# One level of Strassen for the linear layer and for the product of the squares, with the sums spread over GpSimd and ScalarE

## The chip, the cores and the metric

The kernel runs on one core of one Trainium2 chip. The metric is device time in microseconds, the median of several executions; beside it one execution was taken with the hardware profiler, and all durations below are from that one. The engines are TensorE (PE in the profile, its weight loads are PEld), VectorE (DVE), ScalarE (ACT), GpSimd (POOL) and SyncE (SP, which here only starts transfers).

## The reference, cut to what matters

x is 1024 x 512, `weight` is 64 x 512 x 512 (e, f, m), `lin_w` is 512 x 512, all float32.

```python
out_lin = x @ lin_w.T + lin_b
xv = einsum('bf,efm->bem', x, weight)
zp = einsum('bf,efm->bem', square(x), square(weight))
return out_lin + 0.5 * sum(square(xv) - zp, axis=1)      # over e
```

The sum of zp over e is the one product square(x) @ (sum over e of square(weight)), 1024 x 512 by 512 x 512, as large as the linear layer. The product xv is 64 times as large, and its squares have to be formed before the sum over e.

## The kernel before, in words

**The large product.** The 512 outputs are taken in 16 groups of 32; with 64 values of e a group is a product of x (1024 x 512) with a 512 x 2048 matrix. Each group is done by two levels of Strassen in Winograd's form: seven outer products (`tree`, once for each of 1, 6, 2, 7, 5, 4, 3 in `ORDER`), each again by seven inner products (`product`, L488 to L495), each of which is two matmuls of a 128 x 128 stationary block with a 128 x 512 moving block. In all that is 16 x 7 x 7 x 2 = 1568 matmuls; the profile counts every float32 matmul as two instructions, so 3136.

**The sums around it.** The sums of x's blocks are made once, at the start, by VectorE (`x_sum`, tile `x_all` with seven slots X1 to X7). The sums of the weights' blocks are made in part by transfers that add (`load_more`, issued from GpSimd), in part by GpSimd (`t` tiles, L472 to L479). Results leave PSUM through ScalarE copies and VectorE additions; GpSimd makes additions between two SBUF tiles (`whole`, L288). The finished block of xv is squared on ScalarE and summed over e on VectorE (`finish`), into a tile `acc` of 32 columns for each group, which is stored to a scratch tensor in DRAM (`acc_dram`). The weights are squared on ScalarE and summed over e on VectorE (`w_squares`) into the tile `w2_sum` (512 x 512).

**The two small products.** At the start the linear layer is done while x's sums are still being made: L338 to L360, 4 contraction blocks x 8 row tiles = 32 matmuls of 128 x 512, contraction block by contraction block as x and `lin_w` arrive, in four PSUM tiles (b1, b3 and the two of the ring b2, each of two banks). The four are copied out by ScalarE and stored to a second scratch tensor, `lin_dram`. At the end the product of the squares is done in the same shape: L631 to L642, eight row tiles of four matmuls. Before it x is loaded again into the weight tiles w11 and w12 and turned into -0.5 times its square by four VectorE instructions (L604 to L611); the linear layer's result is added by GpSimd-issued adding transfers onto tiles filled with the bias (L603); `acc` of the 15 stored groups comes back by plain transfers (L599) and is added by VectorE (L613 to L622), that of the last group straight from SBUF (L623 to L626). VectorE then adds PSUM to that (L647) and SP stores each of the eight row tiles (L651).

**The order.** The instructions of every engine are emitted in the order that a planner finds (`Plan.order`): each operation has a cost for each engine, its tiles as dependencies, and PE's order is fixed by keys (`key=`). For the other engines it picks by latest allowed time. Every engine runs its own list strictly in order, waiting on semaphores where it depends on another; DMAs are issued in the same way in SP's list (plain ones) and in POOL's list (adding ones).

Of the kernel before, what the change touches and what calls it, by code (L numbers as in the profile page):

```python
# [12 lines left out]
AF = mybir.ActivationFunctionType  # L13
# [3 lines left out]
P = 128  # L17
G = 2
ORDER = (1, 6, 2, 7, 5, 4, 3)

# [160 lines left out]
def kernel(  # L181
# [138 lines left out]
    for k in range(NK):  # L320
        q, r = divmod(k, KH)
        x0, x1, l = f"oa{q}", f"oa{2 + q}", f"ob{q}"
        nc.sync.dma_start(buf[x0][:, r, :], x_src[:, k, ts(0, H)])
        nc.scalar.dma_start(buf[l][:, r, :], lw_src[:, k, :])
        nc.sync.dma_start(buf[x1][:, r, :], x_src[:, k, ts(1, H)])
        for name in (x0, l, x1):
            landing((name, r), 4.3 + 2.6 * k)


    zero = buf["t1_0"]  # L330
    nc.vector.memset(zero, 0.0)  # L331
    for j in range(2):
        nc.tensor.matmul(  # L333
            buf["b1"][:, j, :], zero[:, 0:P], zero, start=True, stop=True
        )
    plan.add({PE: 4.0}, None, (), ("b1",), key=-2000)

    lin_banks = ["b3", "b1", "b2_0", "b2_1"]  # L338
    for k in range(NK):
        q, r = divmod(k, KH)  # L340
        for g, bank in enumerate(lin_banks):
            h = g // 2
            late = k == NK - 1 and g == 3

            def emit(_, k=k, q=q, r=r, g=g, h=h, bank=bank):
                for j in range(G):
                    nc.tensor.matmul(  # L347
                        buf[bank][:, j, :],
                        buf[f"oa{2 * h + q}"][:, r, ts((g * G + j) % (NB // 2), P)],
                        buf[f"ob{q}"][:, r, :],  # L350
                        start=(k == 0),
                        stop=(k == NK - 1),
                    )

            plan.add({PE: PAIR}, emit, ((f"oa{2 * h + q}", r), (f"ob{q}", r)),
                     (bank,), key=PLACE[5] + 0.5 if late else -1000 + 4 * k + g)
    for g, bank in enumerate(lin_banks):
        o = ("ob2", "ob3", "c_0", "c_1")[g]
        act(buf[o], buf[bank], None, (bank,), (o,))
        dma(lin_dram[:, ts(g, G), :], buf[o], (o,), (("lind", g),))  # L360

    def block4(i):
        return buf[f"X{i}"][:, 0:4, :].rearrange("p (k q) b -> p k (q b)", k=2)

# [10 lines left out]
    for i, n in ((1, "A11"), (2, "A12"), (4, "A22")):  # L375
        act(block4(i), a_ap(n), None, a_parts(n), (f"X{i}",))

    def x_sum(writes, o, a, b, kind, reads, size):

        if kind != "-a - b":  # L380
            costs, emit = two_input(DVE, o, a, b, kind == "a - b", size)
        else:
            costs = two_input(DVE, o, a, b, True, size)[0]

            def emit(_):
                nc.vector.scalar_tensor_tensor(o, a, -1.0, b, ALU.mult, ALU.subtract)

        plan.add(costs, emit, reads, writes, both=True)

    for i, a, b, kind in (  # L390
        (5, "A22", "A21", "a - b"),
        (6, "X5", "A11", "-a - b"),
        (7, "A11", "A21", "a - b"),
        (3, "X6", "A12", "-a - b"),
    ):
        x_sum((f"X{i}",), block4(i), a_ap(a), a_ap(b), kind, a_parts(a, b), 1024)
    for lo, hi in ((0, 1), (1, 7)):
        a11, a21, a12, a22, s1, s2, s4 = (x_all[:, lo:hi, s, :] for s in range(7))
        names = tuple(f"X{i + 1}" for i in range(lo, hi))
        for o, a, b, kind in (  # L400
            (s1, a21, a22, "a + b"),
            (s2, s1, a11, "a - b"),
            (s4, a12, s2, "a - b"),
            (a21, a11, a21, "a - b"),
        ):
            x_sum(names, o, a, b, kind, names, Q * (hi - lo))
    for n in a_buf.values():
        plan.add({SP: 0.0}, None, (), (n,) + tuple((n, r) for r in range(KH)))
    for n in ("ob0", "ob1"):
        plan.add({SP: 0.0}, None, (), (n, (n, 0), (n, 1)))  # L410
# [11 lines left out]
    def load_more(n, src, reads=()):  # L422

        plan.add(
            {POOL: 0.9},
            lambda _: nc.gpsimd.dma_start(buf[n], src, accum_op=ALU.add),
            (n,) + reads, (n,), land=2.5, move=5.5,
        )
# [39 lines left out]
    def tree(s, g, i):  # L468
# [16 lines left out]
        def product(p, b, first):  # L485
            op, name = rhs[p]

            def emit(_):  # L488
                for j in range(G):
                    nc.tensor.matmul(  # L490
                        buf[b][:, j, :], buf[f"X{i}"][:, SLOT[p], ts(j, P)], op,
                        start=first, stop=True, skip_group_check=True,
                    )

            plan.add({PE: PAIR}, emit, (name, f"X{i}", b), (b,), key=7 * s + PLACE[p])  # L495
# [4 lines left out]
        def target(pos):  # L500
            return f"{TARGET[i]}{pos}"

        def early(pos):

            return pos == 3 and i in (2, 7, 4, 3)
# [56 lines left out]
    for g in range(NG):  # L562
# [6 lines left out]
        for idx, i in enumerate(ORDER):  # L569
# [10 lines left out]
            tree(7 * g + idx, g, i)  # L580
        if g + 1 < NG:
            names = tuple((acc_name[g], *k) for k in acc_parts)
            dma(acc_dram[:, :, ts(g, MG)], buf[acc_name[g]], names, names + (("accd", g),))


    for n in ("w11", "w12", "w21", "T1", "T2", w(NG, "w22")):
        for c in range(2):
            buf[n, c] = buf[n][:, c]
        plan.add({SP: 0.0}, None, (), (n, (n, 0), (n, 1)))
    xe = {(h, q): (("w11", "w12")[h], q) for h in range(2) for q in range(2)}  # L590
    last = acc_name[NG - 1]
    edge = M - MG
    acc_all = tuple((n, c) for n in ("T2", w(NG, "w22")) for c in range(2))
    lin_all = tuple((n, c) for n in ("w21", "T1") for c in range(2))
    for (h, q), n in xe.items():
        dma(buf[n], x_src[:, ts(q, KH), ts(h, H)], (), (n,))
    for g in range(NB // G):
        n, a = lin_all[g], acc_all[g]
        dma(buf[a][:, :, 0:edge], acc_dram[:, ts(g, G), 0:edge],  # L599
            tuple(("accd", x) for x in range(NG - 1)), (a,))  # L600
        for j in range(G):
            dma(buf[n][:, j, :], lin_b.partition_broadcast(P), (), (n,), 1.0)
        load_more(n, lin_dram[:, ts(g, G), :], (("lind", g),))  # L603
    for n in xe.values():  # L604
        plan.add(
            {DVE: 1.24},
            lambda _, x=buf[n]: nc.vector.scalar_tensor_tensor(  # L607
                x, x, -0.5, x, ALU.mult, ALU.mult
            ),
            (n,), (n,),  # L610
        )  # L611

    def add_acc(g, lo, hi, a, reads):  # L613
        l = buf[lin_all[g]][:, :, lo:hi]
        plan.add(
            {DVE: 0.15 + 1.09 * (hi - lo) / N},
            lambda _: nc.vector.scalar_tensor_tensor(l, a, 0.5, l, ALU.mult, ALU.add),
            reads + (lin_all[g],), (lin_all[g],),
        )

    for g in range(NB // G):
        add_acc(g, 0, edge, buf[acc_all[g]][:, :, 0:edge], (acc_all[g],))  # L622
    for g in range(NB // G):  # L623
        rows = {0: (2, 3), 1: (4, 5)}[g // 2]
        reads = tuple((last, i, 2 * (g % 2) + c) for i in rows for c in range(2))
        add_acc(g, edge, M, buf[last][:, ts(g, G), :], reads)  # L626
# [3 lines left out]
    w2_parts = tuple(("w2", row, m * MI) for row in range(2) for m in range(M // MI))  # L630
    for g, bank in enumerate(("b3", "b1", "b2_0", "b2_1")):  # L631
        o = acc_all[g]
        h = g // 2
        for j in range(G):
            def emit(_, bank=bank, g=g, h=h, j=j):
                for k in range(NK):
                    nc.tensor.matmul(  # L637
                        buf[bank][:, j, :],
                        buf[xe[h, k // KH]][:, k % KH, ts((g * G + j) % (NB // 2), P)],
                        w2_sum[:, k, :],  # L640
                        start=(k == 0), stop=(k == NK - 1),
                    )  # L642

            plan.add({PE: 2 * PAIR}, emit, (xe[h, 0], xe[h, 1]) + w2_parts,
                     ((bank, j),) + ((bank,) if j == 0 else ()), 
                     key=last_key - 0.5 if (g, j) == (0, 0) else last_key + 1 + 2 * g + j)
            costs, emit = two_input(  # L647
                DVE, buf[o][:, j, :], buf[bank][:, j, :], buf[lin_all[g]][:, j, :], False, 512
            )
            plan.add(costs, emit, ((bank, j), lin_all[g], o), ((o, "out", j),))  # L650
            dma(out_dst[:, g * G + j, :], buf[o][:, j, :], ((o, "out", j),), ())  # L651
# [35 lines left out]
```

## Time and profile before

| | |
|---|---|
| median of 3 runs | 1414.77 us (1414.66 to 1415.5) |
| the profiled execution | 1415.29 us, of which its span from first to last instruction is 1413.5 us |
| PE busy | 1405.5 us, 3268 instructions |
| VectorE, GpSimd, ScalarE busy | 1079.4, 1012.5, 680.6 us |
| linear layer (L347) | 64 instructions, 28.5 us busy, from 5.04 to 35.1 us |
| product of the squares (L637) | 64 instructions, 27.8 us busy, from 1379.3 to 1408.7 us |
| an addition of 128 x 1024 | VectorE 1.22 us, GpSimd 2.36 us at the least |
| an addition of 128 x 512 | GpSimd 1.27 us |
| starting an adding transfer of 1 MB | 0.87 us of GpSimd at the least |

In a line of groups or of the timeline the columns are: (start and) duration in us, engine, line of the code, operation, tile written <- tiles read, shapes, how many (x), and in square brackets how long the engine was idle before and what released it. Where several instructions follow one another they are merged into one line with their count.

### The profile page before, as it was taken

To read this page: it belongs to the slowest core of one execution; us is meant where nothing else is said; L and a number is where in the kernel's file an instruction comes from. 1 tells how busy PE (TensorE), PEld (TensorE's weight loads), DVE (VectorE), ACT (ScalarE), POOL (GpSimd) and SP (SyncE) were. 2 spreads that over 40 slices of the span, in tenths; PEclk is the share of its full clock that TensorE was granted. 3 is DMA by queue.
4 is the path that set the end of the run, shared out by engine and by line. 5 is a ranking of instruction groups with operands and counts; after the bars stand their busy time and mean duration, and the time that the engine had idled before them with its cause. 6 is when DMAs were issued, how large, how long until landed. Compare 5 with 4: busy or idle time off the path is not lost.

```text
span 1413.5 us, 10316 instructions
## 1 busy us (share of the span) xinstructions
PE 1405.5 (99%) x3268; PEld 621.4 (44%) x3268; DVE 1079.4 (76%) x933; ACT 680.6 (48%) x696; POOL 1012.5 (72%) x693
## 2 busy tenths in 40 slices
PE   9999999999999999999999999999999999999998
PEld 4444444444444444444444444444444444444443
DVE  6588695877959687696867869687795968769785
ACT  2446364544636355463544636454463644536331
POOL 3686786968678686777958678686877868678660
PEclk9999999999999999999999999999999999999999
DMA  7184472917538183572908447292663818357263
GB/s 267 60 205 122 119 182 67 241 53 175 156 95 206 48 221 91 140 184 79 230 30 195 136 116 185 59 246 56 166 165 90 212 41 213 107 126 181 54 178 90
DMA packets 47638, 197.55 MB, mean 140 GB/s; under 512 B 19040, under 2 KB 20064, under 8 KB 25696
## 3 DMA queue, kind: packets, MB, share of 16 engines
q0 software_dynamic: 11664, 82.84, 30.4%
q1 hardware_dynamic: 35344, 112.99, 22.7%
q10 hardware_dynamic: 576, 1.05, 0.2%
q8 instruction: 27, 0.44, 0.1%
q14 instruction: 27, 0.22, 0.1%
HBM read 173.93 MB, written 6.16 MB: 127 GB/s over the span
## 4 chain that ended last, share of the span: by engine, by line
PE 99%; DVE 1%; issue 0%; DVEq 0%
PE b L490 95%; PE b L347 2%; PE b L637 2%; DVE w L607 0%; PE b L333 0%; DVE oa L284 0%; DVE acc L305 0%; DVE w22a L284 0%; DVEq L683 0%; DVE t L331 0%
## 5 line engine op out<-in xcount | busy, mean ns | idle before, releaser
L490 PE MATMUL b<-t,x_all 128*128 128x512 f32 x1792 | 806.1, 592 | 1.7 <-DVE oa L284 1.7
L490 PEld LDWEIGHTS b<-t,x_all 128*128 128x128 f32 x1792 | 340.3, 190 | 430.7 <-issue 423.6
L490 PE MATMUL b<-w,x_all 128*128 128x512 f32 x768 | 358.1, 592 | 0.0
L284 POOL TENSOR_TENSOR t<-w 128x512 f32<-128x512 f32 x128 | 172.3, 1346 | 163.0 <-PE b L490 93.4
L296 ACT COPY p<-b 128x1024 f32<-128x1024 f32 x160 | 160.9, 1006 | 151.2 <-PE b L490 151.2
L490 PEld LDWEIGHTS b<-w,x_all 128*128 128x128 f32 x768 | 145.9, 190 | 183.7 <-issue 172.7
L284 POOL TENSOR_TENSOR t<-w,t 128x512 f32<-128x512 f32 x128 | 174.1, 1360 | 66.7 <-PE b L490 66.5
L298 ACT ACTIVATE oa<-oa 128x1024 f32<-128x1024 f32 x128 | 133.7, 1057 | 152.7 <-DVE oa L284 152.0
L305 DVE TENSOR_REDUCE acc<-oa 128x16 f32<-128x1024 f32 x128 | 153.8, 1212 | 36.8 <-ACT oa L298 36.8
L490 PE MATMUL b<-T,x_all 128*128 128x512 f32 x384 | 180.4, 592 | 0.0
L305 DVE TENSOR_REDUCE w_sum<-wsq 128x16 f32<-128x1024 f32 x128 | 154.8, 1211 | 25.3 <-ACT wsq L298 25.3
L296 ACT COPY b<-b 128x1024 f32<-128x1024 f32 x112 | 111.9, 999 | 124.7 <-PE b L490 124.7
L284 DVE TENSOR_TENSOR oa<-b,p 128x1024 f32<-128x1024 f32 x96 | 117.1, 1220 | 37.7 <-PE b L490 37.7
L298 ACT ACTIVATE wsq<-w 128x1024 f32<-128x1024 f32 x96 | 98.0, 1056 | 74.3 <-DVE w_sum L305 70.0
L284 POOL TENSOR_TENSOR t<-T 128x512 f32<-128x512 f32 x64 | 91.7, 1433 | 58.1 <-issue 33.1
L284 DVE TENSOR_TENSOR ob<-b,p 128x1024 f32<-128x1024 f32 x48 | 58.6, 1221 | 71.8 <-PE b L490 71.8
L490 PEld LDWEIGHTS b<-T,x_all 128*128 128x128 f32 x384 | 73.0, 190 | 91.8 <-issue 91.8
L298 ACT ACTIVATE c<-c 128x1024 f32<-128x1024 f32 x64 | 66.0, 1056 | 95.4 <-POOL c L284 67.5
L284 DVE TENSOR_TENSOR p<-b,p 128x1024 f32<-128x1024 f32 x80 | 97.6, 1220 | 18.0 <-PE b L490 18.0
L284 POOL TENSOR_TENSOR t<-T,t 128x512 f32<-128x512 f32 x64 | 81.3, 1271 | 20.2 <-PE b L490 20.2
L284 POOL TENSOR_TENSOR c<-oa,p 128x1024 f32<-128x1024 f32 x32 | 89.3, 2791 | 0.1
L284 POOL TENSOR_TENSOR ob<-ob,p 128x1024 f32<-128x1024 f32 x32 | 89.3, 2789 | 0.0
(58 smaller groups left out, 1320.6 us busy)
## 6 DMA issues: line engine op xcount, KB each, us to landing
w<-weight SPq DMA_DIRECT2D x48, 1024.0 KB, 4.9
T<-weight POOLq DMA_DIRECT2D x45, 1024.0 KB, 8.6
T<-weight SPq DMA_DIRECT2D x30, 1024.0 KB, 7.1
w<-weight POOLq DMA_DIRECT2D x16, 1024.0 KB, 11.1
w<-T POOLq DMA_DIRECT2D x16, 1024.0 KB, 6.9
w22a<-weight SPq DMA_DIRECT2D x8, 1024.0 KB, 8.1
w22b<-weight SPq DMA_DIRECT2D x8, 1024.0 KB, 8.1
oa<-xT SPq DMA_DIRECT2D x8, 256.0 KB, 5.4
```

Of the source, the lines that this page charges most:

```text
L284: f(o, a, b)
L296: nc.scalar.copy(o, i)
L298: nc.scalar.activation(o, i, func)
L305: lambda _: nc.vector.tensor_reduce(o, i.rearrange("p a (m e) -> p a m e", e=E), axis=AX.X, op=ALU.add),
L347: nc.tensor.matmul(buf[bank][:, j, :], buf[f"oa{2 * h + q}"][:, r, ts((g * G + j) % (NB // 2), P)], buf[f"ob{q}"][:, r, :], start=(k == 0) ...
L490: nc.tensor.matmul(buf[b][:, j, :], buf[f"X{i}"][:, SLOT[p], ts(j, P)], op, start=first, stop=True, skip_group_check=True,)
L637: nc.tensor.matmul(buf[bank][:, j, :], buf[xe[h, k // KH]][:, k % KH, ts((g * G + j) % (NB // 2), P)], w2_sum[:, k, :], start=(k == 0), st ...
```

## The change

Both small products are done by one level of the same seven-product scheme: x in blocks of 512 x 256, the right-hand matrix in blocks of 256 x 256. A block product (`big_product`) is 8 matmuls of a 128 x 128 stationary block with a moving block of 256 columns, so 56 matmuls of 256 columns stand in place of 32 of 512.

- Linear layer: the left-hand blocks and their sums are those which the large product needs anyway; x and `lin_w` are loaded in another order (first the upper half of x, all four contraction blocks; the lower half after it). The sums of `lin_w`'s blocks (`column_sums`) are four VectorE additions. Two ScalarE copies carry product 1 from PSUM to PSUM, five more bring products out, and three VectorE additions (`lin_last`) complete the results. The last half of product 7 comes after the first inner product of the first tree, as a part of the linear layer did before.
- The first group takes its trees in the order 1, 2, 6, 7, 5, 4, 3.
- Product of the squares: x is squared by ScalarE. Its four block sums (128 x 1024) and the four sums of `w2_sum`'s blocks (128 x 512) are made by GpSimd, into slots of `x_all` that are no longer used. The factor -0.5 moves to the additions at the end.
- Each stored `acc` is halved in place by ScalarE (128 x 256, once for each of the 15 groups), and added to the output tile by four adding transfers from `acc_dram`, where plain transfers and VectorE additions stood. The linear layer's result is added by four such transfers as before. These eight move blocks of four rows of 256 columns per partition, 1 KB at a piece, where the four before moved two rows of 512 columns, 4 KB in one piece.
- VectorE: seven additions from PSUM of 128 x 1024, the last in two halves. The output is stored in five transfers.

```diff
 ORDER = (1, 6, 2, 7, 5, 4, 3)
+ORDER_0 = (1, 2, 6, 7, 5, 4, 3)
...
+    for h, order in enumerate(((0, 1, 2, 3), (2, 3, 0, 1))):
+        for at, k in enumerate(order):
+            q, r = divmod(k, KH)
+            n, l = f"oa{2 * h + q}", f"ob{q}"
+            nc.sync.dma_start(buf[n][:, r, :], x_src[:, k, ts(h, H)])
...
+            if h == 0:
+                nc.scalar.dma_start(buf[l][:, r, :], lw_src[:, k, :])
...
+    def column_sums(engine, b, t, reads, names):
+
+        for k, x, y, r in (
+            (1, b[1], b[0], (0, 1)),
+            (2, b[3], t[1], (3, "t1")),
+            (3, b[3], b[1], (3, 1)),
+            (4, b[2], t[2], (2, "t2")),
+        ):
+            costs, emit = two_input(engine, t[k], x, y, engine == POOL, 512)
...
+    def big_product(bank, lhs, rhs, first, keys, by_k=False):
+
+        (a, a_names), (b, b_names) = lhs, rhs
+        steps = [(u, [k]) for k in range(KH) for u in range(G)]
+        for (u, ks), key in zip(steps if by_k else [(u, range(KH)) for u in range(G)], keys):
+            def emit(_, u=u, ks=ks):
+                for j in range(2):
+                    for k in ks:
+                        nc.tensor.matmul(
+                            buf[bank][:, u, ts(j, HM)],
+                            a[:, k, ts(2 * u + j, P)],
+                            b[:, k, :],
+                            start=first and j == 0 and k == 0,
+                            stop=k == KH - 1,
+                            skip_group_check=True,
+                        )
...
+    lin_product(1, "b2_0", True, -1000, by_k=True)
+    for u in range(G):
+        act(buf["b2_1"][:, u, :], buf["b2_0"][:, u, :], None, (("b2_0", u),), (("b2_1", u),), 0.56)
+    lin_product(2, "b2_0", False, -999, by_k=True)
+    act(buf["ob2"], buf["b2_0"], None, both_halves("b2_0"), ("ob2",))
+    lin_store("ob2", 0, 0)
+    lin_product(4, "b1", True, -998)
+    act(buf["c_0"], buf["b1"], None, both_halves("b1"), ("c_0",))
+    lin_product(5, "b3", True, -997)
+    act(buf["c_1"], buf["b3"], None, both_halves("b3"), ("c_1",))
+    lin_product(6, "b2_1", False, -996)
+    act(buf["ob3"], buf["b2_1"], None, both_halves("b2_1"), ("ob3",))
+    lin_product(3, "b3", False, -995)
+    act(buf["c_2"], buf["b3"], None, both_halves("b3"), ("c_2",))
+    lin_last("ob3", "c_2", -1)
+    lin_store("ob3", 0, 1)
+    lin_product(7, "b2_1", False, -994, last=PLACE[5] + 0.5)
+    lin_last("c_1", "b2_1", -1)
...
-            dma(acc_dram[:, :, ts(g, MG)], buf[acc_name[g]], names, names + (("accd", g),))
+            a = buf[acc_name[g]]
+            plan.add({ACT: 0.4}, lambda _, a=a: nc.scalar.mul(a, a, 0.5), names, names)
+            dma(acc_dram[:, :, ts(g, MG)], buf[acc_name[g]], names, names + (("accd", g),), 0.9)
...
+    for h, c in blocks:
+        n, rows = lin_all[h, c], ts(h, NB // 2)
+        for j in range(NB // 2):
+            dma(quarter(buf[n])[:, j, :], lin_b[ts(c, HM)].partition_broadcast(P), (), (n,), 0.5)
+        load_more(n, lin_dram[:, rows, ts(c, HM)], (("lind", h, c),), 2.7, quarter)
+        load_more(n, acc_dram[:, rows, c * HM:c * HM + edge[c]],
+                  tuple(("accd", x) for x in range(NG - 1)), 2.7,
+                  lambda ap, w=edge[c]: quarter(ap)[:, :, 0:w])
     for n in xe.values():
-        plan.add(
-            {DVE: 1.24},
-            lambda _, x=buf[n]: nc.vector.scalar_tensor_tensor(
-                x, x, -0.5, x, ALU.mult, ALU.mult
-            ),
-            (n,), (n,),
-        )
+        act(buf[n], buf[n], AF.Square, (n,), (n,), 1.07)
...
+    for p, a, b, kind in (
+        (5, a21, lhs[4], "a + b"),
+        (6, 5, lhs[1], "a - b"),
+        (7, lhs[1], a21, "a - b"),
+        (3, lhs[2], 6, "a - b"),
+    ):
...
+        x_sum((f"R{i}", f"X{i}", f"Y{i}"), block4(i), a[0], b[0], kind, a[1] + b[1], 1024, POOL)
...
+    column_sums(POOL, w2_quad, zt, w2_names, zt_names)
...
+    zp_product(1, bank_a, True, -0.9)
+    for u in range(G):
+        act(buf[bank_2][:, u, :], buf[bank_a][:, u, :], None, ((bank_a, u),), ((bank_2, u),), 0.56)
+    zp_product(5, bank_3, True, 1)
+    add_part(1, 1, bank_3, False)
+    zp_product(6, bank_2, False, 2)
+    add_part(0, 1, bank_2, False)
+    zp_product(2, bank_a, False, 3)
+    add_part(0, 0, bank_a, True)
+    zp_product(7, bank_2, False, 4)
+    add_edge(1)
+    add_part(1, 1, bank_2, True)
+    add_part(1, 0, bank_2, False)
+    zp_product(3, bank_3, False, 5)
+    add_edge(0)
+    add_part(0, 1, bank_3, True)
+    zp_product(4, bank_b, True, 6)
+    add_part(1, 0, bank_b, True, True)
```

Here `lin_product` and `zp_product` call `big_product` with the named product's two operands, `lin_store` stores a block to `lin_dram`, `add_part` adds -0.5 times a PSUM tile to the output tile and stores it where told, and `add_edge` adds half of the last group's `acc`. `b1`, `b3`, `b2_0` and `b2_1` (`bank_a`, `bank_3`, `bank_2`, `bank_b`) are the four PSUM tiles.

## The prediction

> **What bounds the kernel now.** I read the page's busy times first, then the chain that ended last, then who waited for whom, then the timeline at both ends. The page and the chain:
>
> ```profile
> PE 1405.5 (99%) x3268; PEld 621.4 (44%) x3268; DVE 1079.4 (76%) x933; ACT 680.6 (48%) x696; POOL 1012.5 (72%) x693
> ...
> PE 99%; DVE 1%; issue 0%; DVEq 0%
> ```
>
> ```profile
> 5.24 26.44 PE b L347 x60
> 31.68 1.72 PE b L490 x4
> 33.40 1.72 PE b L347 x4
> 35.11 1294.38 PE b L490 x3016
> ...
> 1330.66 4.99 DVE w L607
> ...
> 1338.05 41.44 PE b L490 x96
> 1379.49 3.43 PE b L637 x8
> 1382.92 1.72 PE b L490 x4
> 1384.64 24.05 PE b L637 x56
> ```
>
> PE is the bound from end to end, at a granted clock of 1.00: 3016 instructions in 1294.38 us are 429.2 ns each, and nothing else fits between them. So a matmul removed from PE's list is worth its full 0.86 us, as long as PE is then not kept waiting. The only wait of PE behind its first instruction is one of 1.7 us in the waits:
>
> ```profile
> PE b L490 <- DVE oa L284: 1.7, 1, 1.7
> ```
>
> It stands at 1338.05. VectorE was late because one of its four squarings (L607) took 4.99 us instead of 1.2 to 1.3, beside GpSimd additions.
>
> **Matmuls: the gain.** Each small product goes from 64 instructions of 512 columns to 56 matmuls = 112 instructions of 256 columns. The trace has none of 256. From below the price is half of 429.2 = 214.6 ns. From above it is set by the weight loads, which double in number:
>
> ```profile
> 1338.02 0.30 PEld L490 LDWEIGHTS b<-t,x_all 128*128 128x128 f32 x2 [2.51 <-POOL t L284]
> 1338.56 0.19 PEld L490 LDWEIGHTS b<-t,x_all 128*128 128x128 f32 x1 [0.24 <-issue]
> ```
>
> A load takes 0.19 us, and two together cover 0.30, so the second starts 0.11 behind the first; in steady work a load starts with the matmul ahead of it and has 0.24 us to spare. With 256 columns it would still have 0.215 - 0.19 = 0.025. The Trainium skill speaks against this (TensorE: Matmul & The Clock Gate): its "Back-to-back issue gap" says that in a stream of loads and matmuls the spacing is set by both (81 ns where the isolated gap is 56, for 128 columns), and its "The mechanism" that a load overlaps a matmul only in another row group. The second would put 0.11 us on each of 2 x 112 instructions, 24 us, and the change would lose; but then 429.2 ns could not hold here either, since two passes of 512 at 2.4 GHz already fill 426.7. The first would put some 25 ns on each, 5.6 us in all. The page's isolated form, N/2.4 + 2.5, fits 429.2, so for two passes of 256 I take 215.8 ns: 112 x 0.2158 = 24.17 us a product.
>
> - Linear layer before: 26.44 + 1.72 = 28.16, of which 28.16 - 64 x 0.4292 = 0.69 belongs to the first instructions at a slow clock (their loads take 0.34 instead of 0.19 until 6.6 us). After: 24.17 + 0.69 = 24.86. Gain 3.30.
> - Squares before: 3.43 + 24.05 = 27.48. After 24.17. Gain 3.31.
> - The 1.71 us wait: the squarings leave VectorE for ScalarE (4 x 1.06; it is idle for 26.8 of the 46.6 us from 1338.05 to 1384.64). Gain 1.71.
>
> Together 8.32 us.
>
> **The start: can PE be fed?** Before, no matmul but the first waited for data; now PE goes through the upper half of x and all of `lin_w` in 7 us.
>
> ```profile
> 7.71 1.28 ACT L296 ACT_TABLE_LOAD   x1 [7.71 <-DMA oa<-xT]
> 9.09 1.23 DVE L284 TENSOR_TENSOR x_all<-oa,oa 128x1024 f32<-128x1024 f32 x1 [7.68 <-DMA oa<-xT]
> ```
>
> These two waits end when 768 KB and 1024 KB have come on SP's queue, with as much on ACT's beside it; the moved bytes by microsecond (27, 215, 303, 393, 332, 330, 404 KB from 1 us on) put both 0.9 us behind the data. By this rule the contraction blocks land at 4.8, 6.2, 7.7 and 9.0 us. PE needs them at 5.2, 7.6, 9.4 and 11.1: no wait. Product 2 must wait for ScalarE to carry product 1 away: x's first block lands at 6.2, table load 1.28, copy 1.05, free at 8.5; PE's first half is done at 8.5, the copy (0.56) ends near 9.2, PE wants it at 9.4; the second half 0.15 us ahead likewise. Product 4 (12.8) waits for the fourth sum of `lin_w`: VectorE makes three 0.42 us sums behind ScalarE's copy and three of 0.69, 8.5 + 1.3 + 2.1 = 11.9. Product 5 needs a sum of x at 13.5 (PE 16.3), 6 and 3 theirs at 16.0 and 17.2 (PE 19.7, 23.2). Later VectorE stands at the addition behind product 7 until 31.9 with half of T2's sum queued behind it; T2's sum then ends near 34.3, GpSimd's first difference from it near 35.6, and PE takes that at 45.5. The new tree order asks for w21 second, which lands before T2 is summed. I put 0.2 us down (0 to 1.5), for the margins of 0.15.
>
> The 15 halvings of `acc` (about 0.4 us each, by ScalarE's 1.0 us for 1024) lie in ScalarE's idle half; the stored results and bias loads in DMA time before 1360. If a halving came ahead of a PSUM copy that PE waits for, it would cost 0.4 once.
>
> **The end: GpSimd.** Here lies the risk. Its list before:
>
> ```profile
> 1365.71 1.30 POOL L284 TENSOR_TENSOR t<-w22b,t 128x512 f32<-128x512 f32 x1
> 1366.93 1.74 POOL L426 DMA_DIRECT2D T<-lind  x2
> 1368.07 3.00 POOL L284 TENSOR_TENSOR oa<-p,oa 128x1024 f32<-128x1024 f32 x1
> 1377.53 2.37 POOL L284 TENSOR_TENSOR ob<-p,ob 128x1024 f32<-128x1024 f32 x1 [6.47 <-DVE p L284]
> 1379.84 1.77 POOL L426 DMA_DIRECT2D w<-lind  x2
> ```
>
> It is done at 1381.6 with gaps. I walked the new list against PE's (in the old times, where PE's last stretch begins at 1384.64). From 1345.4, when the sum of w21's columns can start (PE takes it at 1348.6; its adding transfer is started near 1333.4 and needs at most 11.3 us as before), GpSimd has no gap: 10 additions of 512 at a pitch of 1.24, 10 of 1024 at 2.32 (1355.22, 1357.54, 1359.86 in the timeline), 7 transfer starts at 0.87. That is 12.4 + 23.2 + 6.1 = 41.7, so the last addition of the last tree ends at 1387.1 instead of 1379.9. Behind it hang ScalarE's square (1.06), VectorE's reduction (1.21), `add_edge` (0.3) and the addition that empties b2_0 (1.22); block product 7 writes b2_0 at 1384.64 + 3 x 3.45 = 1395.0. So GpSimd may be done as late as 1391.0: 3.9 us to spare. All operands that PE takes from it before (sums of x and of `w2_sum`) end by 1381, ahead of their products.
>
> Unknown is what starting a transfer in 1 KB pieces costs. The near rows: 0.87 us for 1 MB in 8 KB pieces and 0.84 for 512 KB in 4 KB pieces, both 128 pieces; now there are 512. From below 0.87; from above, all of it per piece, 3.5. The Trainium skill points both ways: DMA: Bandwidth & Descriptors ("Anatomy of one DMA — SWDGE (gpsimd) path") says that many descriptors go out before more of them cost time, but Perfetto Trace Analysis ("DMA Instruction — SWDGE (GPSIMD)") says that the row ends when the last one is written, so the row is just this work. With 0.87 GpSimd ends at 1387.1, with 3.5 at 1387.1 + 7 x 2.63 = 1405.5, and PE waits 14.5 us. The row has no trend with bytes, so I stay near it: 1.3, that is +3.0. Also the adding transfer of `acc` must wait on the queue until that of the linear layer into the same tile has landed (6.5 to 10.0 us from its start before; in the walked list the second's turn comes 7.7 us behind the first's start): +1, between 0 and 2.3. GpSimd then ends at 1391.1, at the limit. I put 0.4 us down.
>
> The tail behind the last matmul keeps its two VectorE halves (1.29 us) and the last 256 KB store, now in 1 KB instead of 2 KB pieces: 0.2 (0 to 0.5).
>
> **Sum.** 8.32 - 0.2 - 0.4 - 0.2 = 7.5 us. The span 1413.5 becomes 1406.0, the profiled execution 1415.29 becomes 1407.8. It stood 0.52 above the median, so the median 1414.77 becomes 1407.3; I say 1407.2.
>
> **Rivals.**
> 1. GpSimd is late by some us (starts of 1.5 to 2.5 us, or waits on landings): everything beyond 3.9 us of lateness is PE's wait. At 2.0 a start: 7.9 + 1 - 3.9 = 5.0 us in place of the 0.4, so 1411.8; in all 1408.5 to 1414. For it: the list without gaps. Against: the 3.9.
> 2. The weight loads show: 5.6 us by the 25 ns above, 1412.8, or a part of it. For it: only 0.025 us to spare. Against: a load needs the array for 0.11.
> 3. No gain at all but a loss: the same GpSimd starts at 2.8 us or more. The 7.9 us that are left of the gain are used up at 2.4 us (7 x 1.54 + 1 - 3.9), and from 2.8 it is slower by over 0.2%; at 3.5, 18.4 + 1 - 3.9 = 15.5 us and 1422. For it: four times as many pieces. Against: two sizes with the same row.
> 4. The start stalls 1 to 3 us (table load, copies, landings): 1408 to 1410.
> 5. All margins hold and the stores cost nothing: 8.3 us, 1406.5, or a little lower.
>
> **How the numbers follow.** Forecast with case 5: 0.58, within 1405.7 to 1408.4. Rival 1: 0.22; rival 2: 0.08; rival 3: 0.05; rival 4: 0.07. What this kernel's measurement can tell from no change is about 0.2%, 2.8 us. Range 1405.4 to 1411.5: above it lie rival 3, most of 2 and the end of 1, 0.14 in all. Faster 0.90, same 0.05, slower 0.05.
>
> **What would show it.** In the changed profile: the block products' matmuls (`big_product`) at 0.216 us each (the chain's pieces of the two products 24 to 25 us); no wait of PE on VectorE near 1336; the first tree reached 3.3 us earlier; GpSimd's starts of `lind` and `accd` transfers with their own duration; a wait of PE, if any, in the last 25 us on VectorE or GpSimd. Starts above 2.0 us, or 256-column instructions above 0.24 us, would make the prediction wrong.

## The result, and the profile after

The changed kernel takes 1408.97 us (median of 6 runs, 1408.17 to 1409.48), the kernel before beside it 1414.97 us (6 runs, 1414.66 to 1415.86). The ratio is 0.9956 with a 95% interval of 0.9943 to 0.9969: 6.0 us faster where 7.5 were forecast. The number lies in the range (1405.4 to 1411.5), but 1.8 us above the point, and above the 1405.7 to 1408.4 that the forecast's own case was given. So at least one term of the sum was wrong.

The profiled execution is the fastest of the six: 1408.17 us, span 1406.4. That matters below, because it flatters the start of the program. The page's busy times first, then the chain that ended last (start, duration, what):

```profile
PE 1398.7 (99%) x3364; PEld 639.1 (45%) x3364; DVE 1079.7 (77%) x929; ACT 693.4 (49%) x721; POOL 1039.1 (74%) x706
```

```profile
5.05 3.65 PE b L405 x16
...
8.72 0.58 ACT b L299
...
9.35 1.14 PE b L405 x4
...
10.57 0.58 ACT b L299
...
11.19 18.40 PE b L405 x84
29.59 1.72 PE b L580 x4
31.31 1.73 PE b L405 x8
33.03 1342.43 PE b L580 x3128
1375.47 3.45 PE b L405 x16
1378.92 1.72 PE b L580 x4
1380.64 20.93 PE b L405 x96
```

PE is still the bound. The trees (L580) now run from 33.03 to 1375.47 in one piece: the 1.7 us of VectorE in the middle of the old chain is gone. The 256-column instructions (L405) in an unbroken stretch cost 3.45 / 16 = 0.2156 us and 1.73 / 8 = 0.216 us. New on the chain are two ScalarE copies inside the linear layer. The waits say the same (engine and line that waited, for whom, us in total, times, longest):

```profile
PE b L405 <- ACT b L299: 1.4, 2, 0.7
```

These are the two copies of product 1 from PSUM to PSUM that the forecast had ending 0.15 us ahead of PE. The copies' own lines are in the second block; in the first, PE's:

```profile
9.35 1.13 PE L405 MATMUL b<-ob,oa 128*128 128x256 f32 x4 [0.66 <-ACT b L299]
11.19 2.86 PE L405 MATMUL b<-ob,oa 128*128 128x256 f32 x12 [0.71 <-ACT b L299]
```

```profile
8.72 0.57 ACT L299 COPY b<-b 128x512 f32<-128x512 f32 x1 [0.25 <-PE b L405]
10.57 0.57 ACT L299 COPY b<-b 128x512 f32<-128x512 f32 x1 [1.28 <-PE b L405]
```

The first half of product 1 is complete about 0.86 us before the second. Yet the copy of that first half starts at 8.72, behind the last matmul of the whole product (5.05 + 3.65 = 8.70). The copy of the second half, whose data are just as ready at 8.70, starts at 10.57, behind PE's next four instructions (9.35 + 1.14 = 10.49), which only write the other half. ScalarE was not what held it, since its first copy had ended at 9.30. So both copies wait for whatever PE wrote last into the two-bank tile, not for their own half. The semaphore counts in the built program say so too: the first copy waits for all eight matmuls of product 1, the second also for the two that follow.

At the other end, GpSimd's list had been the risk. Its timeline, with the duration that each record shows:

```profile
1342.56 1.29 POOL L516 DMA_DIRECT2D w22a<-lind  x1
1343.39 1.76 POOL L287 TENSOR_TENSOR t<-w,t 128x512 f32<-128x512 f32 x1
...
1376.20 3.85 POOL L516 DMA_DIRECT2D w22a<-accd  x1
1377.00 4.37 POOL L516 DMA_DIRECT2D T<-accd  x1
1377.77 5.97 POOL L287 TENSOR_TENSOR oa<-p,oa 128x1024 f32<-128x1024 f32 x1
1380.09 5.97 POOL L287 TENSOR_TENSOR ob<-p,ob 128x1024 f32<-128x1024 f32 x1
```

The records overlap: the next one begins about 0.8 us behind a transfer start, but from then on every record is longer. An addition of 128 x 1024 shows 2.36 us before the first start, and 5.97 us behind seven of them, 3.65 us more than the 2.32 us pitch. So a start costs 0.8 us of the list's pitch and 0.5 us (3.65 / 7) of a lag that piles up, 1.3 us together. That the lag is real is seen in those who wait: ScalarE's square of the last result but one starts at 1383.78, with the end of that addition's record (1377.77 + 5.97 = 1383.74), and its square of the last one at 1386.10 (1380.09 + 5.97 = 1386.06). What hangs on them is VectorE's work ahead of block product 7. It waits for the first of the two squares, and from there on it has no gap, so the last addition but one sets the time and the last one has about 1 us to spare:

```profile
1384.87 1.22 DVE L308 TENSOR_REDUCE acc<-oa 128x16 f32<-128x1024 f32 x1 [1.99 <-ACT oa L301]
...
1389.59 1.22 DVE L757 SCALAR_TENSOR_TENSOR T<-b,T 128x1024 f32<-128x1024 f32 x1
```

The second line is the addition that empties the PSUM tile for product 7; it ends at 1390.81. PE's timeline of block products 2 and 7:

```profile
1387.38 3.62 PE L405 MATMUL b<-w_sum,w 128*128 128x256 f32 x16
1390.95 3.69 PE L405 MATMUL b<-x_all 128*128 128x256 f32 x16
```

At 3.45 us for a block product, product 7 would have begun at 1390.83. It began 0.12 us late, 0.14 us behind the end of VectorE's addition, and took 0.07 us longer; PE's last stretch is 20.93 us, where 20.73 is what it takes without a wait (as several runs below have it). GpSimd's list ended with nothing to spare.

### The profile page after: what moved, and what is told of

Its sections match the earlier page's. It is cut to its first block, busy times and chain, and to the rows that moved or that the text cites. A ratio compares the mean times of both kernels' runs of the same rounds, so it can differ in the third digit from the quotient of the medians.

```text
span 1406.4 us, 10559 instructions
## 1 busy us (share of the span) xinstructions
PE 1398.7 (99%) x3364; PEld 639.1 (45%) x3364; DVE 1079.7 (77%) x929; ACT 693.4 (49%) x721; POOL 1039.1 (74%) x706
## 4 chain that ended last, share of the span: by engine, by line
PE 99%; DVE 0%; ACT 0%; DVEq 0%; issue 0%; ACTq 0%
PE b L580 96%; PE b L405 4%; PE b L337 0%; ACT b L299 0%; DVE w22a L757 0%; DVEq L820 0%; DVE t L335 0%; ACTq L299 0%
## 5 line engine op out<-in xcount | busy, mean ns | idle before, releaser
L580 PE MATMUL b<-t,x_all 128*128 128x512 f32 x1792 | 805.9, 592 | 0.0
L580 PEld LDWEIGHTS b<-t,x_all 128*128 128x128 f32 x1792 | 340.4, 190 | 427.8 <-issue 422.4
L580 PE MATMUL b<-w,x_all 128*128 128x512 f32 x768 | 358.1, 592 | 0.0
L287 POOL TENSOR_TENSOR t<-w 128x512 f32<-128x512 f32 x128 | 177.1, 1384 | 155.4 <-PE b L580 86.5
L580 PEld LDWEIGHTS b<-w,x_all 128*128 128x128 f32 x768 | 145.9, 190 | 183.3 <-issue 172.9
L287 POOL TENSOR_TENSOR t<-w,t 128x512 f32<-128x512 f32 x128 | 177.1, 1384 | 62.7 <-PE b L580 62.7
L301 ACT ACTIVATE oa<-oa 128x1024 f32<-128x1024 f32 x124 | 129.7, 1057 | 139.0 <-DVE oa L287 136.1
L580 PE MATMUL b<-T,x_all 128*128 128x512 f32 x384 | 180.4, 592 | 0.0
L308 DVE TENSOR_REDUCE acc<-oa 128x16 f32<-128x1024 f32 x124 | 149.0, 1211 | 38.7 <-ACT oa L301 38.7
L299 ACT COPY b<-b 128x1024 f32<-128x1024 f32 (+1 forms) x116 | 114.2, 985 | 125.1 <-PE b L580 120.8
L301 ACT ACTIVATE c<-c 128x1024 f32<-128x1024 f32 x68 | 70.1, 1056 | 92.4 <-POOL c L287 63.0
L580 PEld LDWEIGHTS b<-T,x_all 128*128 128x128 f32 x384 | 73.0, 190 | 91.8 <-issue 91.4
```

The costliest lines, as they stand in the source:

```text
L287: f(o, a, b)
L299: nc.scalar.copy(o, i)
L301: nc.scalar.activation(o, i, func)
L308: lambda _: nc.vector.tensor_reduce(o, i.rearrange("p a (m e) -> p a m e", e=E), axis=AX.X, op=ALU.add),
L580: nc.tensor.matmul(buf[b][:, j, :], buf[f"X{i}"][:, SLOT[p], ts(j, P)], op, start=first, stop=True, skip_group_check=True,)
```

## The experiments

All runs are of the same program with the edit named. Ratios are to runs of the kernel before on the same chip. The changed kernel again, the squarings alone, the old order and the last run with an additional addition were on one chip, the others on a second. Every median is of at least 5 runs.

**The changed kernel again.** No edit.

> The changed kernel itself once more, on the chip of the other runs. 1408.5 to 1409.3, with PE's two waits for ScalarE of 1.4 us together at the start, if what was found in its first profile holds in every execution; if those waits came from an unlucky landing of the operands: fewer or none of them, 1407.5.

1409.12 us (1408.75 to 1409.6), ratio 0.9959 (0.9947 to 0.9972). Both waits are there again, 1.4 us together. Its chain begins differently, though:

```profile
5.31 4.42 PE b L405 x16
...
10.38 1.15 PE b L405 x4
...
12.22 18.40 PE b L405 x84
30.62 1.72 PE b L580 x4
32.34 1.73 PE b L405 x8
34.06 1342.43 PE b L580 x3128
```

Product 1 begins 0.26 us later (5.31 instead of 5.05, here behind the landing of `lin_w`), and its 16 instructions take 4.42 us instead of 3.65, so the trees begin in earnest at 34.06 instead of 33.03. This execution is the typical one (1409.12, span 1407.4), and the accounts below are made with it. The longer part of the difference, 0.77 us, is the slow start of PE that the last section tells of.

**The copies sooner.** ScalarE's two half copies are put into the program directly behind the matmuls that they read; each engine's own order is unchanged.

```diff
-        act(buf["b2_1"][:, u, :], buf["b2_0"][:, u, :], None, (("b2_0", u),), (("b2_1", u),), 0.56)
+        act(buf["b2_1"][:, u, :], buf["b2_0"][:, u, :], None, (("b2_0", u),), (("b2_1", u),), 0.56, soon=True)
```

> The two ScalarE copies that carry product 1 from PSUM to PSUM are emitted directly behind the matmuls they read, so that each waits for its own half and not for one step more; the order on every engine stays as it is. Theory (each copy waits for one PE step too many): the first copy starts when ScalarE is free at 8.5 us and ends at 9.05, PE waits some 0.35 us in place of 1.37 in all, the time falls by 1.0 us to 1408.0. Rival (ScalarE's table load and copy, or landings, hold the copies): they start as before, within 0.2 us of 1409.0.

1409.24 us (1409.14 to 1411.27), ratio 0.9963 (0.9950 to 0.9975): nothing gained. The waits are still 1.4 us; the chain shows that they only moved:

```profile
5.24 3.91 PE b L405 x12
...
9.18 0.58 ACT b L299
...
9.80 1.15 PE b L405 x4
```

PE now stops after 12 instructions of product 1 instead of 16. The first copy no longer waits for the second half's matmuls; in exchange these wait for the copy, since they write the tile that it reads. So the place in the program was not the cause. The tie is to the tile.

**Without the half copies.** The tie is taken away: product 2 gets a tile of its own, product 1 stands in the tile that products 6 and 7 add to, and VectorE adds the two for the first quarter of the result.

```diff
-    lin_product(1, "b2_0", True, -1000, by_k=True)
-    for u in range(G):
-        act(buf["b2_1"][:, u, :], buf["b2_0"][:, u, :], None, (("b2_0", u),), (("b2_1", u),), 0.56)
-    lin_product(2, "b2_0", False, -999, by_k=True)
-    act(buf["ob2"], buf["b2_0"], None, both_halves("b2_0"), ("ob2",))
+    lin_product(1, "b2_1", True, -1000, by_k=True)
+    act(buf["ob2"], buf["b2_1"], None, both_halves("b2_1"), ("ob2",))
+    lin_product(2, "b2_0", True, -999, by_k=True)
+    lin_last("ob2", "b2_0", 1)
```

> The changed kernel, but in the linear layer product 2 is written into a PSUM tile of its own (b2_0) and product 1 into the one that products 6 and 7 add to (b2_1), so ScalarE's two half copies from PSUM to PSUM are gone; VectorE adds product 2 to the copied product 1 instead (one more addition from PSUM, 1.2 us, and one ScalarE copy fewer). Theory (the 1.37 us by which PE waited for these copies come from their being tied to the whole tile; without the tie PE runs through): product 2 follows product 1 without a wait, the linear layer ends about 1.4 us earlier, median about 1407.6. Rival (VectorE's additional 1.2 us makes a sum of x or lin_w late, so the wait only moves on to product 4 or 5): 1408.5 to 1409.5. Rival (the start is limited by the landing of the operands, and PE waits for those instead): 1408.5 to 1409.

1407.17 us (1406.8 to 1407.76), ratio 0.9945 (0.9931 to 0.9959), 7.6 us below the kernel before (1414.74): a little better than expected, and about what the forecast had for the whole change. Its chain and its only wait behind the start:

```profile
1.68 7.68 DMA oa<-xT
...
9.50 19.23 PE b L405 x88
...
30.44 1.73 PE b L405 x8
32.17 1342.43 PE b L579 x3128
```

```profile
PE b L405 <- DMA oa<-xT: 0.8, 1, 0.8
```

In this execution PE began early (5.03), was done with product 1 at 8.72, and now stood for x's third contraction block, which came at 9.36. So where PE starts fast the data are next in line, and the copies' wait hid a part of that landing. The rival of the landing is thus seen here as well, with 0.8 us in this execution; the one with the additional addition below, which has the same linear layer and a slow start (32 instructions in 8.10 us, where two products at full speed take 6.90), has no wait at all.

**Whole pieces.** The scratch tensors for `lin` and `acc` are laid out so that six of the eight adding transfers consist of 128 pieces of 4 KB instead of 512 of 1 KB.

```diff
-    acc_dram = dram.tile([P, NB, M], F32, tag="accd", name="accd")
-    lin_dram = dram.tile([P, NB, M], F32, tag="lind", name="lind")
+    acc_dram = dram.tile([P, 2, NB, M // 2], F32, tag="accd", name="accd")
+    lin_dram = dram.tile([P, 2, NB, M // 2], F32, tag="lind", name="lind")
```

> Both scratch tensors are laid out by half of the columns, so that six of the eight adding transfers read 4 KB in one piece per partition (128 pieces) and only two keep 512. Orders stay. Theory[...]: GpSimd's last additions of 128 x 1024 take 2.4 to 3.5 us in the record in place of 5.97, its list ends some 2.5 us earlier, VectorE's addition ahead of block product 7 has 2 us to spare; the time falls by 0.1 to 0.7 us, 1408.3 to 1408.9, as that product waited 0.12 us at least. Rival (an adding transfer costs so much whatever its pieces): records as in the changed kernel, 1409.0.

1408.55 us (1408.36 to 1408.61), ratio 0.9955 (0.9942 to 0.9967), within the expectation. In time it is hardly to be told from the changed kernel; the profile tells more:

```profile
1342.94 0.86 POOL L516 DMA_DIRECT2D w22a<-lind  x1
1343.54 1.56 POOL L287 TENSOR_TENSOR t<-w,t 128x512 f32<-128x512 f32 x1
...
1379.89 4.50 POOL L287 TENSOR_TENSOR ob<-p,ob 128x1024 f32<-128x1024 f32 x1
...
1381.01 20.73 PE b L405 x96
```

The first start shows 0.86 us instead of 1.29 and the next record begins 0.6 us behind it instead of 0.8, the lag at the end is 4.50 - 2.32 = 2.2 us instead of 3.65, and GpSimd's last addition of the tree ends 1384.39 - 1381.01 = 3.4 us behind the start of PE's last stretch instead of 1386.06 - 1380.64 = 5.4. That is 2.0 us more room, 0.4 us for each of the five starts in this stretch that became whole (of the other transfers two keep 512 pieces, and one is started earlier). PE's last stretch is 20.73 us, so the 0.2 us is gone, and no more, since no more was lost.

**One more addition.** To the changed kernel, one GpSimd addition of 128 x 1024 (2.32 us) is added behind the last sum of the squares.

```diff
+        if op is behind:
+            for _ in range(1):
+                nc.gpsimd.tensor_add(block4(5), block4(5), block4(5))
```

> One more GpSimd addition of 128 x 1024 (2.3 us, on a block that nobody reads any more) behind the last sum of x squared. Theory (GpSimd's list at the end has nothing to spare): block product 7 waits for VectorE 2.3 us longer, 1411.2. Rival (3.9 us are spare, as the prediction reckoned): 1409.0.

1410.51 us (1410.31 to 1410.78), ratio 0.9969 (0.9957 to 0.9981), 1.5 us above the changed kernel, and the wait stands where the forecast had put it:

```profile
PE b L405 <- DVE T L758: 1.8, 1, 1.8
```

```profile
1376.92 4.36 POOL L796 TENSOR_TENSOR x_all<-x_all 128x1024 f32<-128x1024 f32 x1
1378.75 3.79 POOL L516 DMA_DIRECT2D w22a<-accd  x1
```

The added addition (L796) lengthens GpSimd's list by 1.83 us, not by the 2.32 of its neighbours, and the whole of it comes out as PE's wait. So the changed kernel has no room at the end. The expected 1411.2 was too high since it counted 2.3 us.

**The three edits together.** Whole pieces, the copies sooner at the start, and the same for the copies and the last halves in the product of the squares.

> Copies emitted early, scratch tensors in whole pieces, and the two halves of the last VectorE addition emitted behind their own half of the last block product. If the theories of the first two runs hold and the last half costs 0.65 us less behind the last matmul: 1.0 + 0.65 + 0.1 to 0.7 us less, 1406.6 to 1407.3. If only the tail counts: 1408.3.

1410.56 us (1410.2 to 1412.19), ratio 0.9972 (0.9962 to 0.9983): a miss, and slower than the changed kernel. PE waits for ScalarE three times (2.6 us) and once for VectorE (0.8 us): the earlier place in the program brings the tie to the whole tile also to the end, where the changed kernel had no such wait. The longest of the three is at the start, and there ScalarE itself was late:

```profile
9.50 1.13 PE L405 MATMUL b<-ob,oa 128*128 128x256 f32 x4 [1.21 <-ACT b L299]
```

PE stood from 8.29, but ScalarE's table load and its copy of x lasted until 8.96. So here the first half copy would have been about 0.35 us late even without the tie to the tile (an estimate: PE's other four instructions would have ended at 8.29 + 0.86 = 9.15, and the copy let PE go on at 9.50). Three of the seven runs took 1412.05 to 1412.19; why is not shown.

**Without the half copies, with whole pieces.** The two edits above that each did what they should.

> The kernel without the half copies in the linear layer, and in addition the parts of lin and acc stored so that six of the eight adding transfers have 128 pieces of 4 KB instead of 512 of 1 KB. Theory (two separate losses: 1.4 us at the start, and no margin at the end): 1407.0 to 1407.5, with GpSimd's last additions at least 2 us earlier against PE's last stretch. Rival (the end costs nothing, as the run with whole pieces alone gained only 0.4 us): equal to the run without the half copies within 0.3 us.

1407.18 us (1406.28 to 1407.66), ratio 0.9944 (0.9930 to 0.9959): equal to the one without whole pieces. The rival is right. The room at the end is there (VectorE stands idle for 1.90 us ahead of the addition behind block product 2), but hardly anything wants it: PE's last stretch is 20.73 us instead of 20.87.

**And one more addition.** The same, with the additional GpSimd addition.

> The kernel without the half copies and with whole pieces, and in addition one more addition of 128x1024 on GpSimd (2.32 us) behind the last sum of the squares, as in the run that added it to the changed kernel. In the profile without the addition VectorE stands 1.90 us idle ahead of the addition that follows block product 2, and block product 7 is released some 2 us before PE wants it. Theory (whole pieces give about 1.8 us of margin at the end): 1407.4 to 1407.8, PE's wait 0.5 us at most. Rival (the pieces' size gives no margin; the addition costs as much as in the changed kernel, 1.5 us): 1408.7.

1406.54 us (1406.38 to 1407.7), ratio 0.9943 (0.9931 to 0.9956). The addition that cost the changed kernel 1.5 us costs nothing here; PE's last stretch is 20.73 us and there is no wait at all. With the run before it, this shows the whole pieces to be worth about 2 us of room and at most 0.2 us of time. It is also the fastest of all medians, but that is not the addition's doing: its 5 runs and those of the kernel without it overlap.

**The linear layer alone.** The product of the squares and the end as in the kernel before.

> Only the linear layer by Strassen; the product of the squares with all eight block products, VectorE's squarings and the end as in the kernel before. If the parts add up as the two profiles have them (linear layer 2.1 us shorter in place of the 3.1 forecast, the wait of 1.7 us behind the squarings stays): median 1412.9. If the forecast's 3.1 us of the start is right and the profile of the changed kernel was unlucky in its start: 1411.9.

1411.83 us (1411.42 to 1412.45), ratio 0.9979 (0.9971 to 0.9987). The number fits the second expectation and its reason is a third one. The linear layer itself gained only 0.94 us: the trees begin at 34.17 instead of 35.11, after a slow start. The rest is the wait of 1.7 us behind VectorE's squarings, which is not there, though the squarings are:

```profile
1321.13 1.25 DVE L703 SCALAR_TENSOR_TENSOR w<-w 128x1024 f32<-128x1024 f32 x1
...
1326.90 1.22 DVE L703 SCALAR_TENSOR_TENSOR w<-w 128x1024 f32<-128x1024 f32 x1
```

```profile
34.17 1342.43 PE b L580 x3128
```

None of the four takes longer than 1.25 us. In the kernel before, the one that took 4.99 began at 1330.66, with GpSimd's addition of the same instant:

```profile
1330.66 2.66 POOL L284 TENSOR_TENSOR oa<-p,oa 128x1024 f32<-128x1024 f32 x1
1332.99 1.56 POOL L284 TENSOR_TENSOR t<-T 128x512 f32<-128x512 f32 x1
```

and was over 1.1 us behind the end of the second of these (1335.65 and 1334.55), about the time of one squaring. In the new order no squaring meets such a pair. Two of them meet a single addition, and there it is GpSimd's that takes longer. The first line is from this run, beside the squaring at 1321.13; the second is the same addition in the next run, which has the squarings on ScalarE:

```profile
1321.30 3.29 POOL L287 TENSOR_TENSOR ob<-ob,oa 128x1024 f32<-128x1024 f32 x1
1321.30 2.34 POOL L284 TENSOR_TENSOR ob<-ob,oa 128x1024 f32<-128x1024 f32 x1
```

The one beside the squaring at 1326.90 takes 2.34 us instead of 1.28, and the first squaring of the kernel before (1322.07) has such a neighbour too, of 3.30 us. So in four meetings one of the two engines was held up, three times GpSimd by about 1 us and once VectorE by 3.8; PE felt only the last. That the one that is held up stands until the other is done would fit all four, but it was not tried by itself.

**The squarings alone.** The kernel before, with its four squarings on ScalarE; the factor -0.5 goes into VectorE's last additions.

```diff
-        plan.add(
-            {DVE: 1.24},
-            lambda _, x=buf[n]: nc.vector.scalar_tensor_tensor(
-                x, x, -0.5, x, ALU.mult, ALU.mult
-            ),
-            (n,), (n,),
-        )
+        act(buf[n], buf[n], AF.Square, (n,), (n,), 1.07)
```

> The kernel before, with only its four squarings of x moved from VectorE to ScalarE (the factor -0.5 goes into VectorE's last additions); all eight block products, the old linear layer. Forecast's term: the wait of 1.71 us on VectorE goes, 1413.0. Rival (the wait is the accident of one squaring that meets two GpSimd additions and comes and goes with the order of the lists, so that the move itself buys it only by chance): still 1413.0 here, since no squaring is left to meet them; if the wait has another cause: 1414.7.

1413.2 us (21 runs, 1412.32 to 1413.91), ratio 0.9987 (0.9981 to 0.9994), 1.8 us below the kernel before. The trees run in one piece of 1342.43 us. So a third of the whole change's gain can be had without the new block products, by moving four instructions; and by the run before, also with the squarings left on VectorE, in an order in which they fall elsewhere.

**The squares alone.** The linear layer as in the kernel before.

> Only the product of the squares by Strassen, with the squarings on ScalarE, the halving of acc and the adding transfers; the linear layer as in the kernel before. If the parts add up as the two profiles have them (squares 3.1 us, and the wait of 1.7 us gone): median 1410.1 to 1410.3. If the wait would have come back without the earlier start of the trees, or GpSimd's list has less room: 1411 to 1412.

1410.29 us (1409.75 to 1410.39), ratio 0.9966 (0.9953 to 0.9979), as expected. With the linear layer alone, the two parts give 4.45 + 2.91 = 7.4 us, where the whole gives 5.9 to 6.0: each of them removes the same wait of 1.7 us, which counts once. What is left, 5.4 to 5.7 us, is 0.2 to 0.6 us short of the whole; that rest is not explained, and the start alone can differ by as much from one execution to the next.

**The old order of the first group.** One edit of the diff undone.

```diff
-        order = ORDER if g else ORDER_0
+        order = ORDER
```

> The changed kernel with the trees of the first group in the old order (1, 6, 2, ...) in place of the new one (1, 2, 6, ...). Theory (T2's sum is ready at 37.1 us and GpSimd's first difference from it starts at 37.3 us, where PE would take it in the second tree from about 45 us): no wait, the same as the changed kernel within 0.4 us, 1408.6 to 1409.3. Rival (the order is needed, since the second tree would otherwise wait for T2): 1410 to 1413.

1409.06 us (1408.32 to 1409.25), ratio 0.9958 (0.9946 to 0.9971), the same as the changed kernel. The new order buys nothing here; T2's sum is in time either way.

## Why the prediction was right, and where not

The account is made with the second profile of the changed kernel (span 1407.4) against that of before (1413.5), step by step.

- **256-column instructions** at 215.8 ns: 215.6 to 216.3 measured. The lower bound of 214.6 was a good guide. Of the two rules of the Trainium skill that were weighed (TensorE: Matmul & The Clock Gate, "Back-to-back issue gap" and "The mechanism"), neither shows: with one weight load for each, 215.6 ns leaves no room for 25 ns more, let alone 0.11 us. Rival 2 is out.
- **Linear layer**, gain 3.30: 1.12 (28.15 us before, 4.42 + 1.15 + 18.40 + 1.73 + 1.34 of waits = 27.04 after). Here the prediction failed, at the step "the first half copy ends near 9.2, PE wants it at 9.4; the second half 0.15 us ahead likewise". Each copy was costed as if it depended on its half. It is tied to the tile, so PE waited 0.65 and 0.69 us; the run without the half copies, which has no such tie, gains them back. And a wait costs more than its length: the four instructions behind the first took 1.15 us instead of 0.86, the 84 behind the second 18.40 instead of 18.13. Together 1.34 + 0.56 = 1.9 us where 0.2 was put down. The other 0.28 is the slow clock: 0.69 was taken from before, 4.42 - 3.45 = 0.97 was there. In the first profile it was 0.20; with the start 0.26 us earlier this makes the 1.0 us by which that execution's span is shorter.
- **The landings at the start**: x's third block was put at 7.7 us; in the kernel without half copies it came at 9.36, and another execution of that start has it at 9.07. The rule behind it was read from two transfers and stretched to the others. In the changed kernel the wait for the copies covers it. T2's sum was put at 34.3 us and was ready at 37.1, which does no harm.
- **The wait of 1.71 us**: gone, and worth more than its length by a restart as well (from the start of the trees to that of the squares 1342.44 us instead of 1344.38: 1.94). The effect was right. The reason given, that the squarings leave VectorE, is enough for it (the squarings alone give 1.8 us) but not needed: with the linear layer alone they stay, and the wait goes all the same.
- **Squares**, gain 3.31: 27.48 became 3.45 + 20.93 = 24.38, so 3.10.
- **GpSimd at the end**: 1.3 us for a transfer start, chosen between 0.87 and 3.5, measured 0.8 + 0.5. PE lost 0.2 us where 0.4 was put down. That this fits is in part luck, since two errors of about 1 us cancelled. The last tree's addition was forecast to end 6.5 us behind the start of PE's last stretch (1391.1 against 1384.64) and ended 5.4 behind it: the 1 us put down for waits on landings did not come, as the list has no gap. But the limit was also 1 us nearer than reckoned: the forecast followed only the last addition with 4.0 us of work behind it, where the addition before it and 7.2 us of work behind that (1383.74 to 1390.95), most of it VectorE's unbroken row, set the time. The record of a start is no measure of it, however: the first shows 1.29 us, the last 4.37, while the pitch is 0.8. The Trainium skill (Perfetto Trace Analysis, "DMA Instruction — SWDGE (GPSIMD)") has the record end when the descriptors are written, and the growing records agree with that. What the instruction takes from those behind it is seen only in the pitch and in how far the later records' ends slip. Rivals 1 and 3 are out, rival 3 by a wide margin; but the run with one more addition shows that rival 1 was not far away: every further microsecond would have been PE's.
- **Tail**: 0.2 put down; from the end of PE to the end of the span it is 4.8 us before and after. Nothing.

The sum of the measured steps is 1.12 + 1.94 + 3.10 = 6.2, less 0.07 because PE began that much later, 6.1 of span. The forecast had 7.5. Rival 4 (the start stalls for 1 to 3 us, 1408 to 1410) is what happened, with a chance of 0.07 beside 0.58 for the forecast. That was too little for margins of 0.15 us which rested on two dependencies that had been assumed and not looked up.

## What to carry to other kernels

Before a margin of a few tenths of a microsecond between two engines is believed, look at what the built program's semaphores wait for: a copy of half a PSUM tile was tied to every matmul into either half, and emitting it earlier only turned the wait around, while a tile of its own for each product removed it. A wait of the bound engine that comes from an accident of the order can go with an edit that was made for something else, as here with the linear layer alone; gains that contain it cannot be added up, and it is worth trying whether its cause can be moved by itself. And an engine that ends its list exactly in time is not free: measure its room by adding one instruction, and look up how much longer that made the list.

## What the runs showed of the hardware

**The moment at which TensorE reaches full speed differs from one execution to the next**, with the same first matmul at 1.46 us. Sixteen instructions take 3.45 us in an unbroken stretch at full speed, and 3.69 behind a wait (product 2 of the kernel without half copies, from 9.50 on). Product 1 took 3.65, 3.69, 3.81, 3.95, 4.14, 4.42, 4.43 and 4.60 us in eight profiles (two executions of the changed kernel, and six edits that leave product 1's matmuls as they are), while the granted clock in the page's rows stood at 1.00 in all of them. In the fast ones all weight loads of product 1 take 0.19 us; in the slow ones the first take 0.34. The Trainium skill (TensorE: Matmul & The Clock Gate, "What's actually happening") has the array at half speed until a free-running window of about 3.4 us has been busy; a window that is free-running begins at a different moment in each execution, which would give such a spread. The same section puts the spread of that moment at 500 ns to either side; here the times differ by up to 0.95 us, which at half speed is a shift of some 1.9 us (an estimate), so it is wider than the page has it. The two executions of the changed kernel differ by 0.77 us in product 1, a good part of the 1.3 us between the fastest and slowest of its first six runs, and more than several of the terms that were argued about.

**A wait of TensorE costs its length and 0.2 to 0.3 us more**, which the chain shows in the stretch behind it: 1.15 instead of 0.86 us for four instructions, 18.40 instead of 18.13 for 84, and 41.44 instead of 41.20 for the 96 of 512 columns behind the wait of the kernel before.

**GpSimd's transfer starts leave a lag behind them**: 0.5 us for a start of 512 pieces, 0.3 on the mean (2.18 us over seven starts) where five of seven have 128 pieces, beside the 0.8 and 0.6 us that the pitch of the list shows. The lag piled up over 40 us of a list without gaps and was seen only in the ends of the records and in those who waited for them.
